# Two-layer network on one Trainium2 core: the experts' last layer as seven block products summed over the experts in PSUM

## The chip, the cores and the metric

The kernel runs on one core of one Trainium2 chip, in float32 throughout. The metric is the device time of one execution in microseconds (us), as the median of several runs; smaller is better. A profiled execution gives the times of single instructions on the five engines: PE (TensorE, matrix products; PEld is its weight load), DVE (VectorE), ACT (ScalarE), POOL (GpSimd) and SP (SyncE, which issues transfers). Matrix products land in PSUM, eight banks of 2 KB per partition; VectorE and ScalarE read them there, and everything else lies in SBUF.

## The reference

The input x is 32 x 128 tokens of 256 numbers (4096 tokens). Layer 0 adds a masked attention over all tokens with eight heads. Layer 1, where the change lies, is this:

```python
t = t + attention_in_a_window_of_24(layernorm(t), K)
t = t + experts(layernorm(t))

def experts(x):                                    # batch of one
    w = softmax(x @ Wr + br)                       # 8 shares per token
    h = relu(bn1(einsum('bfd,edh->bfeh', x, W1) + b1))
    h = relu(bn2(einsum('bfeh,ehk->bfek', h, W2) + b2))
    y = einsum('bfeh,ehd->bfed', h, Wo) + bo
    return einsum('bfed,fe->bfd', y, w)            # shares times outputs, summed
```

All eight experts see every token, so each of them is three products with a 256 x 256 matrix, and the last product is weighted by the token's share and summed over the experts.

## The kernel before

**Three stages.** Up to about 743 us runs layer 0's attention (scores L1257, exponentials L1269 and L1271, products L1301, sums L1291). From 743 to 790 us a front written out by hand (lines 2099 to 2203) brings the first block of 512 tokens through layer 1's attention: output projection of layer 0 in two halves (`first_halves`, `second`, `complete`), normalisation, turning, keys, window scores, exponentials, weights, `apply`/`attended`, the second normalisation (`expert_tokens`, L1768), its turning (`turn_tokens`), the first plain layer (`layer_halves`), the router (`route`, L1793). `batch_norms` (L1746) makes the scales and shifts for the experts there; its first step is a square root on ScalarE and a reciprocal (L908, L909). From 790 us on run the experts.

**The expert stage.** The work is 64 units, eight blocks of 512 tokens times eight experts, with the expert in the inner loop: `work = [(b, e) ...]`. A unit has three layers. `Layer(0, ...)` and `Layer(1, ...)` (L1887) hold channels on the partitions and tokens along the free axis. From unit PLAIN = 3 on each is done as a 2 x 2 block product with seven products instead of eight (Strassen's form with fifteen sums): `first()` issues four products of 128x128 by 128x256 into two PSUM banks, a and q (L1898), then a copy on ScalarE (u, L1924) and three additions on VectorE (L1925, L1926, L1927); `last()` adds three more products into the same banks, a relu from bank a on ScalarE (L1883), one addition on VectorE from bank q (L1940, 128x512), and two relus on ScalarE. The sums of weights come from GpSimd (`weight_sums`, L1540) during the first block, are stored to DRAM (`kept_sums`) and loaded again for later blocks (L1524). The sums of tokens for the second layer are three additions on VectorE (`token_sums`, L1873, L1877, L1878), called between the first layer's `last()` and the second layer's.

**The last layer.** `combine(ht, k, r2)` (L1947) is called twice a unit. It uses the second layer's output as weights, so that tokens land on the partitions: four products of 128x128 by 128x256 on TensorE into one bank psy (L1955), then two additions on VectorE that multiply a tile of 128 tokens by its share and add it to the token's residual in SBUF (`scalar_tensor_tensor`, L1963). The last expert's call sends the tile out.

**Order.** The main loop (L2359) writes, for unit k: the loads for unit k + 2 on SyncE's queue; first layer of unit k + 1, `first()`; half a combine; second layer of unit k, `first()`; `last()` of the first layer; half a combine; the token sums; `last()` of the second layer. After each piece `insert(passed)` (L2327) puts up to three jobs of later blocks: projections with a bias (`with_bias`, L904, on GpSimd), statistics, normalisation, turning, keys, scores, exponentials, routing, shares, biases. A job has a cost in TensorE time and due times spread over SPAN = E * 9.5 us a block; it comes LATER = 3.2 us of planned time after what it needs. Each engine runs its instructions in the order in which they were written.

**PSUM in this stage.** ps_h has four banks (two layers' a and q), ps_x four (jobs and combine):

```python
ps_h = ctx.enter_context(tc.tile_pool(name="ps_h", bufs=4, space=PSUM))
ps_x = ctx.enter_context(tc.tile_pool(name="ps_x", bufs=4, space=PSUM))
```

**Tokens.** Blocks 4 to 7 of the input are loaded early into tiles of their own (pool `res`) and held.

Of the kernel before, what the change touches and what calls it, by code (L numbers as in the profile page):

```python
# [823 lines left out]
def fast_kernel(ctx: ExitStack, tc: tile.TileContext, ins: dict, out: bass.AP, narrow):  # L824
# [92 lines left out]
    last_parts = []  # L917
    with ExitStack() as l0:
# [296 lines left out]
        with ExitStack() as at:  # L1215
# [4 lines left out]
            ps_a = scores_ps.enter_context(tc.tile_pool(name="ps_a", bufs=1, space=PSUM))  # L1220
            ps_b = scores_ps.enter_context(tc.tile_pool(name="ps_b", bufs=2, space=PSUM))
            ps_av = scores_ps.enter_context(tc.tile_pool(name="ps_av", bufs=1, space=PSUM))
# [160 lines left out]

            stat_at = {
# [17 lines left out]
            for n in range(len(steps) + LAG + 1 + 16):  # L1402
# [22 lines left out]
                if 0 <= n - LAG < len(steps):  # L1425
                    product(*steps[n - LAG])
                    bb, gg, jj = steps[n - LAG]
                    if jj == orders[bb][-1]:
                        ends = bb, gg
                        later.setdefault(n + 1, []).append((close_sums, ends))  # L1430
                        if ends != LASTU:
                            later.setdefault(n + 6, []).append((invert, ends))
                            later.setdefault(n + 12, []).append((scale, ends))
# [46 lines left out]
    res = ctx.enter_context(tc.tile_pool(name="res", bufs=1))  # L1480
# [7 lines left out]


    one_a = ps_a.tile([P, BLK], F32, tag="a", name="one_a")  # L1490
    one_b = ps_av.tile([P, BLK], F32, tag="av", name="one_b")
    three_a, three_b = (
        ps_b.tile([P, HG - 1, BLK], F32, tag="b", name=f"three{k}") for k in range(2)
    )
    ps_h = ps_x = None

    def open_banks():
        nonlocal ps_h, ps_x
        scores_ps.close()
        ps_h = ctx.enter_context(tc.tile_pool(name="ps_h", bufs=4, space=PSUM))  # L1500
        ps_x = ctx.enter_context(tc.tile_pool(name="ps_x", bufs=4, space=PSUM))
# [8 lines left out]
    w12, s12, wo, kept_sums = {}, {}, {}, {}  # L1510
# [15 lines left out]
    def load_last(k):  # L1526
        wo[k] = wf.tile([P, 2, D], F32, tag="wo", name=f"wo_{k}")
        expert_weights(wo[k], "Wo", work[k][1])

    def weight_sums(e):  # L1530

        t = s12[e] = wf.tile([P, 4, 2, P], F32, tag="s12", name=f"s12_{e}")
        a11, a21, a12, a22 = (
            w12[e][:, :, c, m * P : (m + 1) * P] for c in range(2) for m in range(2)
        )
        for k, (p, q, op) in enumerate((
            (a21, a22, ALU.add), (t[:, 0], a11, ALU.subtract),
            (a11, a21, ALU.subtract), (a12, t[:, 1], ALU.subtract),
        )):
            nc.gpsimd.tensor_tensor(t[:, k], p, q, op=op)  # L1540
        kept_sums[e] = wdr.tile([P, 4, 2, P], F32, name=f"kept{e}")
        nc.sync.dma_start(out=kept_sums[e], in_=t)

    Ksb = l1c.tile([P, 2, D], F32, name="Ksb")
    nc.sync.dma_start(out=Ksb, in_=ins["L1_attn_K"].rearrange("(c p) e -> p c e", p=P))
    load_tokens(4, res.tile([P, TPB, D], F32, name="tokens4"))
# [14 lines left out]
    def load_rest():  # L1561
        load_tokens(TPB + 1, res.tile([P, TPB, D], F32, name=f"tokens{TPB + 1}"))
        load_layers(1)
        for b in range(TPB + 2, NBLK):
            load_tokens(b, res.tile([P, TPB, D], F32, name=f"tokens{b}"))
# [7 lines left out]
    def deviations(ts, part):  # L1573
# [8 lines left out]
        nc.vector.reciprocal(rstd0[:, cols], rstd0[:, cols])  # L1582
        nc.vector.scalar_tensor_tensor(
# [10 lines left out]
    def project_half(n, c, ps, start):  # L1594
        nc.tensor.matmul(
            ps, lhsT=big_t[:, c, SIDE + n * P : SIDE + (n + 1) * P], rhs=woT[:, c, :],
            start=start, stop=(c == 1), skip_group_check=True,
        )

    def project(n):  # L1600
        ps = bank(f"pso{n}")[:, :D]
        for c in range(2):
            project_half(n, c, ps, not c)
        finish(n, ps)
        if n + TPB < NTILE:
            with_bias(n + TPB)
# [92 lines left out]
    def turn_weights(p, ps=None):  # L1699
# [11 lines left out]
        nc.vector.tensor_copy(pt[: 4 * SIDE, 2, :], ps[: 4 * SIDE, 2 * P : 3 * P])  # L1711
# [33 lines left out]

    def batch_norms():  # L1746
        def bnp(s):
            k = bn_names.index(s) * 2 * E
            return bnT[:, :, k : k + 2 * E]

        rstd_of(bscale, bnp("v"), 1e-3)
# [35 lines left out]
    def route(b):  # L1787

        xfT = blk[b]["xfT"]
        ps = bank(f"psr{b}")[:, :P]  # L1790
# [36 lines left out]
    def turn_shares(b):  # L1827
        ps = bank(f"pswt{b}")[:, :P]
        nc.tensor.transpose(ps, blk[b]["wide"].rearrange("p r e -> p (r e)"), ident)
        blk[b]["wT"] = fx.tile([P, P], F32, tag="wT", name=f"wT{b}", bufs=1)  # L1830
        nc.vector.tensor_copy(blk[b]["wT"], ps)
# [38 lines left out]
    def token_sums(x, tag, name):  # L1870

        t = fh.tile([P, 4, HB], F32, tag=tag, name=name)
        nc.vector.tensor_tensor(  # L1873
# [3 lines left out]
        nc.vector.tensor_tensor(t[:, 2], x[:, 1, HB:], t[:, 0], op=ALU.subtract)  # L1877
        nc.vector.tensor_tensor(t[:, 3], x[:, 1, :HB], t[:, 2], op=ALU.subtract)  # L1878
# [8 lines left out]
    class Layer:  # L1887
# [21 lines left out]
        def first(self):  # L1909
# [8 lines left out]
            self.product(a[:, 0], w[:, 0, :P], x[:, 0, :HB], True)  # L1918
            self.product(q[:, 0], s[:, 0], t[:, 0], True)
            self.product(a[:, 1], s[:, 1], t[:, 2], False)  # L1920
# [25 lines left out]

    def combine(ht, k, r2):  # L1947
        b, e = work[k]
        w = blk[b]["w"]
        dst = out[0].rearrange("n t d -> (n t) d")  # L1950
# [9 lines left out]
        for i in range(2):  # L1960
# [6 lines left out]
            if e == E - 1:  # L1967
                nc.sync.dma_start(out=dst[n * P : (n + 1) * P], in_=tokens(n))
# [11 lines left out]
    def bound_squares(name):  # L1980
        squares[name] = l1c.tile([P, 2, D], F32, tag="sq", name=f"sq_{name}", bufs=2)
        nc.gpsimd.tensor_tensor(squares[name], bound_of[name], bound_of[name], op=ALU.mult)
# [113 lines left out]
    def half(ps, k):  # L2096
        return ps[:, k * D : (k + 1) * D]

    def first_halves(n, ps, k):

        project_half(n, 0, half(ps, k), not k)


    places = [
        (one_a, 0), (one_a, 1), (one_b, 0), (one_b, 1),
        (three_a[:, 0], 0), (three_a[:, 0], 1), (three_a[:, 1], 0), (three_a[:, 1], 1),
    ]
    for n, (ps, k) in enumerate(places):
        first_halves(n, ps, k)

    def second(n):
        project_half(n, 1, half(*places[n]), False)

    def complete(n):
        finish(n, half(*places[n]))

    invert_last, scale_last = last_parts
    second(0)
# [9 lines left out]
    second(4)  # L2128
    complete(4)
# [10 lines left out]
    warm(one_b, 20)  # L2140
# [10 lines left out]
    complete(TPB + 1)  # L2151
    complete(TPB + 2)

    three_b = ps_b.tile([P, HG - 1, BLK], F32, tag="b", name="three_b")
    for n, (ps, k) in enumerate(((1, 0), (1, 1), (2, 0), (2, 1)), 2 * TPB):
        places.append((three_b[:, ps], k))

    def both(n):
        first_halves(n, *places[n])
# [3 lines left out]
    rows = [(one_a, 0), (one_a, 1), (three_b[:, 0], 0), (three_b[:, 0], 1)]  # L2163
    seen = [scores1(i, half(*rows[i])[:, :BW]) for i in range(TPB)]
    for n in range(2 * TPB + 1, 3 * TPB):
        both(n)
    for i in range(TPB):
        seen[i]()
        exponentials(i)
        if i == 1:  # L2170
            turn_weights(0, one_b)
    complete(2 * TPB - 1)
    attended = apply(0, [one_a[:, :D], one_b[:, :D]])
    turn_weights(1, three_a[:, 0])
    batch_norms()
    attended(0)
    attended(1)
    deviations(range(0, 2), 0)
    attended = apply(1, [one_a[:, :D], one_b[:, :D]])
    deviations(range(0, 2), 1)  # L2180
    expert_tokens(0, 0)
    turn_tokens(0, 0, three_a[:, 1])
    attended(0)
    attended(1)
    deviations(range(2, TPB), 0)
    a = layer_halves(blk[0]["xfT"], [one_b, three_a[:, 0]])
    next(a)
    deviations(range(2, TPB), 1)
    expert_tokens(0, 1)
    turn_tokens(0, 1, one_a)  # L2190
# [3 lines left out]
    a = next(a)  # L2194
    open_banks()
    deviations(groups[1], 1)
    route(0)
    first_free = 3 * TPB
    for n in range(first_free, first_free + TPB):
        with_bias(n)  # L2200
# [11 lines left out]
    for n in groups[0]:  # L2212
        done_at["normalise", n] = done_at["turn", n] = -9
    for g in (0, 1):
# [9 lines left out]
    for b in range(1, NBLK):  # L2224
        ts = groups[b]
        for n in ts:
            job(("project", n), 0.86, lambda n=n: project(n))
# [29 lines left out]
        job(("devt", b), 0, lambda b=b: deviations(tiles(b), 1), ("devt0", b))  # L2257
# [16 lines left out]
        if b == 2:  # L2274
            two_ahead = {"wV": "wc", "K": "wK"}
            for name in bound_of:
                job(
                    ("square", name), 0, lambda name=name: bound_squares(name),
                    *((("columns", two_ahead[name]),) if name in two_ahead else ()),
                )  # L2280
# [21 lines left out]
    SPAN = E * 9.5  # L2302
# [4 lines left out]
    for name, cost, f, needs in jobs:  # L2307
        own = isinstance(name, tuple) and isinstance(name[1], int)
        b = name[1] if own else 2
        if own and name[0] in ("project", "normalise", "turn"):  # L2310
# [16 lines left out]
    def insert(passed):  # L2327

        nonlocal now, spent
        now += passed  # L2330
# [16 lines left out]
    known = set(done_at) | {j[0] for j in jobs}  # L2347
# [3 lines left out]
    h1, h2 = {0: (a, None)}, {}  # L2351
    halves = [(k, r2) for k in range(len(work)) for r2 in range(2)]
    sums_of = {0: (0, 1), 1: (2, 3)}

    def combine_half():
        k, r2 = halves.pop(0)
        combine(h2[k], k, r2)

    for k in range(len(work)):  # L2359
        if k + 2 < len(work):  # L2360
            load_layers(k + 2)
        load_last(k)
        if k + 2 < E:
            for e in sums_of.get(k, (k + 2,)):
                weight_sums(e)
        one = None
        if k + 1 < len(work):
# [5 lines left out]
            insert(1.73)  # L2373
        if k >= 2:
            combine_half()
            insert(1.73)
        two = Layer(1, k, *h1.pop(k))
        two.first()
        insert(1.73)
        if one:  # L2380
            one.last()
# [59 lines left out]
```

## Time and profile before

| what | value |
|---|---|
| median of 3 runs | 1539.02 us (1538.96 to 1543.28) |
| profiled execution, time | 1543.32 us |
| profiled execution, span on the core | 1541.5 us |
| granted TensorE clock, mean | 0.991 |
| TensorE busy | 1484.6 us, 8877 instructions |
| bytes moved | 110.16 MB, mean 71 GB/s |

The span is the profiled execution's own; 1.8 us lie around it. Busy times of engines overlap. A product of 128x128 by 128x256 in float32 shows as two instructions of 0.38 us that overlap, so its slot is read from the distance of starts, not from the mean duration. A row of the timeline names the start, the time until the last of its instructions ended, the engine, the line, the operation, output and inputs, and, in brackets, for how long the engine had been idle and which instruction ended that. Line numbers are those of the kernel before.

### The profile page before, as it was taken

How to read it: one execution, taken by the hardware profiler on the slowest of the kernel's cores; microseconds unless marked ns; L12 is line 12 of the kernel's file. 1: busy time of each engine (PE TensorE's matmuls, PEld its weight loads, DVE VectorE, ACT ScalarE, POOL GpSimd, SP SyncE). 2: the span in 40 equal slices, each digit the busy share in tenths (PEclk: the TensorE clock that was granted, in tenths of full speed). 3: DMA queues.
4: the chain of work that ended last, by engine and by line, in shares of the span. 5: the costliest groups of instructions: out<-in, count | busy, mean ns of one | idle time of the engine just before them, and what ended most of it. 6: DMA issues, size and time to landing. Idle time of an engine off the chain costs nothing.

```text
span 1541.5 us, 23828 instructions
## 1 busy us (share of the span) xinstructions
PE 1484.6 (96%) x8877; PEld 840.7 (55%) x8877; DVE 1204.5 (78%) x2203; ACT 937.4 (61%) x1393; POOL 162.0 (11%) x380
## 2 busy tenths in 40 slices
PE   8899899999999999999889999999999999999998
PEld 5333232222222222222547878887877888888887
DVE  3677888989999898999647778677777777777775
ACT  3676687878888888988444445545454444544443
POOL 1111003000000000031053002001010010000000
PEclk8999999999999999999989999999999999999999
DMA  4211101010000010000322333343333433343441
GB/s 117 56 31 27 39 8 31 8 29 9 1 15 8 1 49 15 8 9 1 115 79 93 116 117 106 115 139 107 116 107 112 141 107 117 106 141 111 137 151 64
DMA packets 95976, 110.16 MB, mean 71 GB/s; under 512 B 17527, under 2 KB 84846, under 8 KB 95854
## 3 DMA queue, kind: packets, MB, share of 16 engines
q1 hardware_dynamic: 93008, 106.61, 22.4%
q8 instruction: 72, 1.18, 0.3%
q10 hardware_dynamic: 1150, 1.09, 0.3%
q0 software_dynamic: 1696, 0.87, 0.2%
q14 instruction: 50, 0.41, 0.1%
HBM read 98.87 MB, written 8.53 MB: 70 GB/s over the span
## 4 chain that ended last, share of the span: by engine, by line
PE 72%; DVE 15%; ACT 8%; issue 4%; DMA 0%; POOL 0%; DVEq 0%; ACTq 0%; SPq 0%; POOLq 0%
PE psh L1898 17%; PE sa L1257 14%; PE av L1301 13%; PE psy L1955 10%; DVE acc L1291 3%; ACT h L1883 3%; ACT pt L1271 2%; PE psq L995 2%; PE psv L1010 2%; PE psk L982 2%; PE psk L1654 2%; DVE h L1940 1%; PE sb L1257 1%; DVE tokens L1963 1%; PE psh L1903 1%
## 5 line engine op out<-in xcount | busy, mean ns | idle before, releaser
L1291 DVE TENSOR_TENSOR acc<-acc,pt 128x1024 f32<-128x1024 f32 (+3 forms) x500 | 529.4, 1126 | 40.0 <-ACT pt L1271 28.7
L1271 ACT ACTIVATE pt<-sb 128x1536 f32<-128x1536 f32 (+3 forms) x288 | 387.3, 1345 | 3.3 <-PE sb L1257 3.2
L1257 PE MATMUL sa<-q,kT 32*128 32x512 f32 (+3 forms) x576 | 302.2, 604 | 9.4 <-ACT pt L1269 7.1
L1257 PE MATMUL sb<-q,kT 32*128 32x512 f32 (+3 forms) x1728 | 306.1, 604 | 2.2 <-ACT pt L1271 1.1
L1883 ACT ACTIVATE h<-h,bshift,bscale 128x256 f32<-128x256 f32 x244 | 159.2, 699 | 231.6 <-DVE h L1940 231.6
L1301 PE MATMUL av<-pt,v 128*32 128x512 f32 (+3 forms) x2304 | 286.2, 569 | 3.1 <-POOL pt L1275 1.6
L1955 PE MATMUL psy<-wo,h 128*128 128x256 f32 x1024 | 242.9, 380 | 0.0
L1269 ACT ACTIVATE pt<-sa 128x512 f32<-128x512 f32 (+3 forms) x288 | 162.5, 564 | 92.7 <-PE sb L1257 63.1
L1955 PEld LDWEIGHTS psy<-wo,h 128*128 128x128 f32 x1024 | 191.9, 190 | 30.7 <-issue 5.8
L1257 PEld LDWEIGHTS sa<-q,kT 32*128 32x128 f32 x576 | 84.2, 182 | 220.1 <-ACT pt L1269 180.0
L1301 PEld LDWEIGHTS av<-pt,v 128*32 128x32 f32 x2304 | 45.4, 108 | 202.2 <-issue 182.8
L1963 DVE SCALAR_TENSOR_TENSOR tokens<-psy,w,tokens 128x256 f32<-128x256 f32 x256 | 111.1, 475 | 34.2 <-PE psy L1955 33.7
L1925 DVE TENSOR_TENSOR u<-psh,u 128x256 f32<-128x256 f32 x122 | 51.1, 419 | 101.3 <-ACT u L1924 101.2
L1275 POOL MEMSET pt<- 32x128 f32 (+2 forms) x192 | 58.6, 305 | 635.2 <-ACT pt L1271 541.2
L1883 ACT ACTIVATE h<-psh,bshift,bscale 128x256 f32<-128x256 f32 (+1 forms) x132 | 75.9, 575 | 55.5 <-PE psh L1898 41.3
L1257 PEld LDWEIGHTS sb<-q,kT 32*128 32x128 f32 x1728 | 88.0, 182 | 10.2 <-ACT pt L1271 6.8
L1924 ACT COPY u<-psh 128x256 f32<-128x256 f32 x122 | 44.1, 362 | 78.6 <-PE psh L1898 78.5
L1898 PE MATMUL psh<-tx,s 128*128 128x256 f32 x366 | 89.3, 380 | 0.0
L1898 PE MATMUL psh<-th,s 128*128 128x256 f32 x366 | 89.0, 379 | 0.0
L1940 DVE TENSOR_TENSOR h<-psh,u 128x512 f32<-128x512 f32 x122 | 83.1, 681 | 1.5 <-PE psh L1898 1.4
L1898 PEld LDWEIGHTS psh<-tx,s 128*128 128x128 f32 x366 | 69.2, 190 | 10.4 <-DVE h L1940 0.8
L1898 PEld LDWEIGHTS psh<-th,s 128*128 128x128 f32 x366 | 69.5, 190 | 9.5
(316 smaller groups left out, 1785.6 us busy)
## 6 DMA issues: line engine op xcount, KB each, us to landing
w<-in_L_ffn_W_dram SPq DMA_DIRECT2D x128, 256.0 KB
s<-kept SPq DMA_DIRECT2D x56, 512.0 KB
wo<-in_L_ffn_Wo_dram SPq DMA_DIRECT2D x64, 256.0 KB
xg<-in_x_dram SPq DMA_DIRECT2D x32, 128.0 KB
tokens<-in_x_dram SPq DMA_DIRECT2D x8, 512.0 KB
kept<-s SPq DMA_DIRECT2D x8, 512.0 KB
out_dram<-tokens SPq DMA_DIRECT2D x32, 128.0 KB
rec<-flat SPq DMA_DIRECT2D x60, 64.0 KB
```

Of the source, the lines that this page charges most:

```text
L1257: nc.tensor.matmul((sb[:, h - 1, :] if h else sa)[:, lo:], lhsT=kT[rows, g, j * P : (j + 1) * P], rhs=q[rows, g, lo:], start=True, stop=True,)
L1269: nc.scalar.activation(pt[:, 0, lo:], sa[:, lo:], AF.Exp, scale=SCALE)
L1271: nc.scalar.activation(pt[:, 1:, lo:], sb[:, :, lo:], AF.Exp, scale=SCALE)
L1275: nc.gpsimd.memset(pt[k * N : (k + 1) * N, :, lo : lo + k * N], 0.0)
L1291: nc.vector.tensor_tensor(live[b, g][:, hs, lo:], old[:, hs, lo:], pt[:, hs, lo:], op=ALU.add)
L1301: nc.tensor.matmul(av[h * HD : (h + 1) * HD, lo:], lhsT=v[:, j, (g * HG + h) * HD : (g * HG + h + 1) * HD], rhs=pt[:, h, lo:], start=(j == ...
L1883: nc.scalar.activation(dst, src, AF.Relu, bias=bshift[:, m, k : k + 1], scale=bscale[:, m, k : k + 1])
L1898: nc.tensor.matmul(ps, lhsT=w, rhs=x, start=start, stop=True, skip_group_check=True)
L1925: nc.vector.tensor_tensor(u, a[:, 1], u, op=ALU.add)
L1940: nc.vector.tensor_tensor(flat.rearrange("p (k c) -> p k c", k=2), self.q, self.u.unsqueeze(1).to_broadcast([P, 2, HB]), op=ALU.add,)
L1955: nc.tensor.matmul(ps[:, i, :], lhsT=ht[:, c, r * P : (r + 1) * P], rhs=wo[k][:, c, :], start=(c == 0), stop=(c == 1),)
L1963: nc.vector.scalar_tensor_tensor(out=tokens(n), in0=ps[:, i, :], scalar=w[:, r, e : e + 1], in1=tokens(n), op0=ALU.mult, op1=ALU.add,)
```

## The change

For units 0 to 61 (SUMMED = 62) the last layer becomes a 2 x 2 block product of seven products too, and its eight experts are summed in PSUM:

- **Shares first.** The shares are written to DRAM per block, and for every unit one row is broadcast to all partitions (`load_shares`, SyncE). GpSimd multiplies the second layer's output by it (`shared`: two products of 128x512) and makes the three token sums.
- **Seven products a unit**, issued one at a time by `product()`, up to four between the four pieces of a unit's order (`between`), into four banks that stay for a whole block (`ps_y`). The sums of Wo's blocks are made once by VectorE (`last_sums`) and reloaded later.
- **Once per block** `close_block` forms the four quarters from the seven sums (one ScalarE copy, six VectorE additions), and `turn_out` turns the result back to tokens on the partitions (eight transposes), adds the residual and sends it out. Units 62 and 63 keep `combine`.
- **PSUM:** ps_h goes from 4 banks to 2, ps_x from 4 to 2, ps_y gets 4. In `first()` the second product of bank a now comes before the first of bank q.
- **Order:** `one.first, between, one.last, between, two.first, between, two.last, between`; SPAN = E * 9.05; `with_bias` becomes a job; blocks 4 to 7 of the input are loaded again when a block's output is out (`load_again`), in place of `res`.
- **Front:** first halves of the projections are issued ahead of the last product of layer 0; table loads are called up by a one-element activation (`ready`); `batch_norms` is split and later; routing and the first layer come before the completions of tiles 8 to 11; 16 warming transposes in place of 20; only one `with_bias` ahead of the stage.

```diff
+        ps_h = ctx.enter_context(tc.tile_pool(name="ps_h", bufs=2, space=PSUM))
+        ps_x = ctx.enter_context(tc.tile_pool(name="ps_x", bufs=2, space=PSUM))
+        ps_y = ctx.enter_context(tc.tile_pool(name="ps_y", bufs=1, space=PSUM))
...
             self.product(a[:, 0], w[:, 0, :P], x[:, 0, :HB], True)
+            self.product(a[:, 1], s[:, 1], t[:, 2], False)
             self.product(q[:, 0], s[:, 0], t[:, 0], True)
-            self.product(a[:, 1], s[:, 1], t[:, 2], False)
             self.product(q[:, 1], s[:, 2], t[:, 1], False)
...
+    def shared(k):
+        b, e = work[k]
+        wb = blk[b].pop(("wb", e))
+        for c in range(2):
+            nc.gpsimd.tensor_tensor(h2[k][:, c, :], h2[k][:, c, :], wb, op=ALU.mult)
+        return h2[k], token_sums(h2[k], "ty", f"ty{k}", nc.gpsimd)
+    def last_products(k):
...
+        for i, j, lhs, rhs in (
+            (0, 0, w[:, 0, :P], x[:, 0, :HB]), (0, 1, w[:, 1, :P], x[:, 1, :HB]),
+            (1, 0, s[:, 3], x[:, 1, HB:]), (1, 1, s[:, 0], t[:, 0]),
+            (2, 1, s[:, 2], t[:, 1]), (2, 0, s[:, 1], t[:, 2]),
+            (3, 0, w[:, 1, P:], t[:, 3]),
+        ):
+            first = not e and (i, j) in ((0, 0), (1, 0), (2, 1), (3, 0))
+            nc.tensor.matmul(
+                y[i][:, j], lhsT=lhs, rhs=rhs, start=first, stop=True, skip_group_check=True
+            )
+            yield
+    def turn_out(b, r2):
+        ps = bank(f"psc{b}_{r2}")
...
+        nc.vector.tensor_tensor(t, ps.rearrange("p (k d) -> p k d", d=D), t, op=ALU.add)
...
+    SHARED, SUMS = 5.0, 7.5
+    def product(forced=False):
...
+        if not forced and now < second_done[k] + (SHARED if i < 3 else SUMS):
+            return False
...
+    def between():
+        product()
+        insert()
+        begin_shared()
+        product()
...
             one.first()
-            insert(1.73)
-        if k >= 2:
-            combine_half()
-            insert(1.73)
+            passed(1.73)
+            if k:
+                between()
+            one.last()
+            passed(1.3)
+            between()
         two = Layer(1, k, *h1.pop(k))
         two.first()
-        insert(1.73)
-        if one:
-            one.last()
-            insert(1.3)
-        if k >= 1:
-            combine_half()
-            insert(1.73)
...
+        between()
         two.last()
...
+        second_done[k] = now
+        between()
```

## The prediction

> **What bounds the kernel now.** I first read the busy shares, then the windows by stage, then the groups of instructions, and last the rows of the expert stage one by one. The first view says which engine is nearest to full:
>
> ```profile
> PE 1484.6 (96%) x8877; PEld 840.7 (55%) x8877; DVE 1204.5 (78%) x2203; ACT 937.4 (61%) x1393; POOL 162.0 (11%) x380
> ```
>
> An average over stages does not price an edit to one stage, so I cut the span where the work changes. The columns are stretch, length, PE, PEld, DVE, ACT, POOL (busy us), granted clock, DMA share, GB/s.
>
> ```profile
> 743.00:790.00 47.00, 36.34 (x177) 25.83 (x176) 31.08 (x98) 14.81 (x32) 9.48 (x17) 0.89 0.31 102
> ...
> 828.50:1425.80 597.30, 589.49 (x2874) 487.13 (x2874) 450.92 (x1191) 278.09 (x561) 45.74 (x102) 1.00 0.36 117
> 1425.80:1514.00 88.20, 87.58 (x407) 75.66 (x406) 64.06 (x148) 40.78 (x76) 0.00 (x0) 1.00 0.44 144
> ```
>
> The first stretch is the hand-written front; the second holds 50 expert units with the next blocks' jobs between them (597.3 / 50 = 11.95 us each); the third has almost no jobs. In both expert stretches PE idles about 1%: TensorE bounds them. A unit without jobs is 22 passes: in the trace a unit's first product starts at 1504.06 and the next unit's at 1513.56, so 9.50 / 22 = 0.432 us a pass. The groups that the change touches:
>
> ```profile
> L1955 PE MATMUL psy<-wo,h 128*128 128x256 f32 x1024 | 242.9, 380 | 0.0
> L1963 DVE SCALAR_TENSOR_TENSOR tokens<-psy,w,tokens 128x256 f32<-128x256 f32 x256 | 111.1, 475 | 34.2 <-PE psy L1955 33.7
> ```
>
> **What TensorE alone would gain.** Units 0 to 61 need seven passes in place of eight: 62 x 0.432 = -26.8 us. Turning eight blocks back adds 64 transposes; four such transposes take 0.43 us in the same stage of this trace, so 64 x 0.109 = +7.0. Net -19.8 us, if TensorE stays the bound.
>
> **What the change takes for it.** The four running sums of a block need four PSUM banks for eight units. So Layer's pool ps_h falls from four banks to two, and one layer needs both. In the changed issue order the next layer's third product (bank q) waits for the sum L1940 of the layer before, and ScalarE's copy L1924 of the next layer stands behind the two relus that wait for that same sum. With four banks two layers are in flight; with two, each layer follows the one before through a closed loop TensorE, VectorE, ScalarE, VectorE. Its links can all be timed in the trace of before, in the tail where nothing else is queued (start, length, engine, operation, idle time before it and what ended it):
>
> ```profile
> 1495.78 0.69 DVE L1940 TENSOR_TENSOR h<-psh,u 128x512 f32<-128x512 f32 x1
> ...
> 1496.50 1.30 ACT L1883 ACTIVATE h<-h,bshift,bscale 128x256 f32<-128x256 f32 x2 [2.00 <-DVE h L1940]
> 1497.71 0.35 ACT L1924 COPY u<-psh 128x256 f32<-128x256 f32 x1
> ...
> 1498.09 0.42 DVE L1925 TENSOR_TENSOR u<-psh,u 128x256 f32<-128x256 f32 x1 [1.63 <-ACT u L1924]
> ...
> 1498.62 0.42 DVE L1926 TENSOR_TENSOR h<-psh,u 128x256 f32<-128x256 f32 x1
> 1499.08 0.42 DVE L1927 TENSOR_TENSOR h<-psh,h 128x256 f32<-128x256 f32 x1
> ```
>
> From the start of L1940 to the end of L1927 are 1499.50 - 1495.78 = 3.72 us. TensorE follows VectorE within about 0.05 us, where it does wait:
>
> ```profile
> 1124.54 0.42 DVE L1927 TENSOR_TENSOR h<-psh,h 128x256 f32<-128x256 f32 x1
> ...
> 1125.02 0.70 PE L1898 MATMUL psh<-xfT,s 128*128 128x256 f32 x2 [0.29 <-DVE h L1927]
> ```
>
> Then come the layer's last two products and the handover to L1940: 0.43 + 0.59 + 0.04 = 1.06 us. The loop is 3.72 + 0.05 + 1.06 = 4.83 us a layer, two layers a unit: 9.66. In every second layer VectorE has the three sums of L1873, L1877 and L1878 between L1927 and L1940; they take 1.52 us (1503.76 to 1505.28) in a gap of 1.11, so +0.41. **A unit without jobs becomes 10.07 us**, against 9.50 before and 21 x 0.432 = 9.07 by TensorE alone.
>
> The Trainium skill ("Perfetto Trace Analysis", section "Matmuls") says independent matmul groups should rotate through PSUM banks so that evacuation of one overlaps the next group's matmuls. The rule speaks against this change, with two groups' banks cut to one's; it gives no price, and no run here yet shows it.
>
> **With jobs between.** TensorE's own need is 11.95 - 0.43 + 0.11 (turning back) = 11.63 us a unit. The loop lengthens by every job operation that stands on ScalarE between relus and copy, or on VectorE between L1927 and L1940. Counted in the issue order of the changed kernel, over 103 layers of units 4 to 55 and by durations of before's rows: 30 us of ScalarE operations (a 128x256 normalise 0.55, exponentials, copies) with some 8 us of table loads (1.28 each); on VectorE 89 us beyond the gaps, of which 21 are the 0.41 above. So 9.66 + (30 + 8 + 89) / 51.5 = 12.1 us. That is a mean; a layer takes the longer of loop and TensorE's passes, which are unevenly spread (4.3 to 6.5 us a layer). Taking the longer one layer by layer, with the same durations, gives 644 / 51.5 = 12.5. Ends: 11.6 (all of it beside other work, TensorE the bound) and 12.7 (every such operation also delays its neighbour). I take **12.35**: 50 x (12.35 - 11.95) = **+20 us**. Nine units without jobs: 9 x 0.57 = **+5**.
>
> **VectorE and GpSimd.** VectorE loses 248 of the L1963 (0.435 each in pairs, 108 us) and gains a block's closing (six operations, some 2.8 us) and eight sums of the last weights. The 108 us were idle cover, not the bound; this gain counts at nothing but for the loop, where it is already left out. GpSimd gets two products of 128x512 and three sums per unit. From its rows (queried by line):
>
> ```profile
> L1982 POOL TENSOR_TENSOR sq_wV<-wVT 128x512 f32<-128x512 f32 x1 | 1.1, 1053 | 0.0
> L1540 POOL TENSOR_TENSOR s<-w,s 128x256 f32<-128x256 f32 x6 | 4.4, 730 | 0.0
> ```
>
> 3 x 1.05 + 2 x 0.73 = 4.6 us of a unit's 10 to 12, where it now does next to nothing: it fits, and the last layer's products are ordered at least 5 us (7.5 for the sums) behind. But one pair of rows shows VectorE losing beside it, an operation of one element per partition at 1.04 us, and 0.16 alone (814.85):
>
> ```profile
> 818.99 1.05 POOL L1982 TENSOR_TENSOR sq_wV<-wVT 128x512 f32<-128x512 f32 x1
> 819.70 1.04 DVE L1690 TENSOR_TENSOR nm<-nm,negt 128x1 f32<-128x1 f32 x1
> ```
>
> VectorE's loop operations read PSUM, and L1963 kept its 0.47 beside the same GpSimd row (820.66). The three sums read SBUF alone, but GpSimd works from 2 to 6.6 us after the second layer's L1940 and the sums stand 8 to 10 us after it. Cost taken: 0; ends 0 and 0.88 x 62 = +55.
>
> The Trainium skill ("SBUF — State Buffer", section "Who interferes with whom") says a VectorE operation with two SBUF inputs and a GpSimd operation that reads SBUF exclude each other for the whole instruction. By it, the sums meeting a GpSimd operation of 1.05 in each of 62 units would make up to +65; the 1.04 us row agrees with the rule.
>
> **DMA.** 62 broadcasts of shares (256 KB) and some 54 reloads of kept sums (256 KB) add 30 MB to 750 us, 40 GB/s to today's 117 at a share of 0.36: near 0.5, no bound. SyncE's queue takes two more issues of 0.4 to 0.9 us a unit. Tokens of blocks 4 to 7 come again only after a block's output has left; with_bias may wait for them on GpSimd with the xh transfers and the share products behind it. Taken 0; ends 0 and 4 x 5 = +20.
>
> **Front.** TensorE idles 10.4 us between 743 and 790, in nine gaps. The largest, 2.79 (until 773.59, behind batch_norms and its table load) and 2.71 (until 789.09, routing behind four completions), are what the reorder removes; two pairs of L1768 took 1.61 and 1.77 beside GpSimd instead of 0.8, about 1.8 more; an earlier table load 0.9. Sum 8.2: **-8**, ends 0 and -12. **End:** the turning back of block 7 and its VectorE closing stand before the last outputs: 0.9 + 2.1 = **+3**, ends 0 and 5. Units 0 to 3 I take at 0, ends -3 and +3.
>
> **Sum.** +20 + 5 - 8 + 3 = +20 on the profiled execution's 1543.3 (span 1541.5 and 1.8 around it), so 1563. That execution was the slowest of its kind, 4.3 above the median 1539.0; on the median's scale the forecast is **1559**.
>
> **Rivals.**
> - *TensorE stays the bound* (faster): where a unit's jobs add under 11.63 - 10.07 = 1.56 us to the loop, the passes hide it. For it: jobs are many, and TensorE needs 11.63 itself. Against: counted, they add 2.1. Then 50 x -0.32 = -16, +5, -8, +3: 1523; if the bare loop also hides, -20 - 8 + 1: 1512.
> - *GpSimd becomes the wait* (slower still): collisions at half the upper price, +28, or products waiting for shares: 1580 to 1600. Against: 4.6 us of 10 and the distance kept.
> - *Nothing to measure*: the loop costs 12.0 us a unit and the front pays for it: 1535 to 1543.
>
> **How the numbers follow.** Forecast (loop-bound; 1544 to 1578 with 12.1 to 12.6 a unit and a front of 0 to -12) 0.56; GpSimd 0.11; no change 0.07; TensorE-bound 0.26. About 0.3% is what a measurement can tell from no change. Faster 0.26, same 0.07, slower 0.67. The range for 8 in 10 reaches 1516 to 1590.
>
> **What would show it.** In the tail without jobs: units of 10.1 us, TensorE waiting for L1927's and L1940's successors twice a unit, copies right behind relus, PE near 90%. If units are 9.1 there, the loop is wrong. With jobs: units over 12 us, PE near 94%. GpSimd's rival shows as products waiting on POOL, or sums over 1 us. The front is right if the first layer product comes 8 us earlier than 789.67 less what stage one moved.

## The result and the profile after

The changed kernel takes 1624.32 us in the median of four runs (1620.61 to 1627.78), the kernel before 1539.45 beside it: 1.0541 times as long, with a 95% interval of 1.0522 to 1.056. The forecast was 1559, the range 1516 to 1590: the side was right, the size too small by 65 us, and the time lies outside the range. The profiled execution took 1620.6 us, its span is 1618.8, so 77.3 more than before's span.

The busy shares of the kernel after:

```profile
PE 1511.1 (93%) x8813; PEld 824.5 (51%) x8813; DVE 1175.5 (73%) x2041; ACT 943.2 (58%) x1404; POOL 487.7 (30%) x691
```

TensorE has 64 instructions fewer and is busy 26.5 us longer. That is the first thing to see here: its work takes more time per instruction. To find where, I cut both traces at four marks that both have: the first layer product of the stage, and the last addition (L1940 before, L1978 after) of the second layer of units 10, 54 and 62. The windows of after, then of before (stretch, length, then PE, PEld, DVE, ACT and POOL busy, granted clock, DMA share, GB/s):

```profile
780.32:961.20 180.88, 152.20 (x632) 107.95 (x633) 109.17 (x280) 67.80 (x133) 90.61 (x107) 0.91 0.37 121
961.20:1515.20 554.00, 519.88 (x2427) 407.74 (x2426) 359.55 (x884) 248.35 (x497) 264.95 (x306) 0.99 0.48 155
1515.20:1599.60 84.40, 79.95 (x341) 62.82 (x340) 46.10 (x97) 35.00 (x66) 41.77 (x40) 0.98 0.51 166
```

```profile
789.67:931.10 141.43, 138.82 (x641) 104.89 (x638) 94.89 (x264) 65.92 (x132) 34.08 (x66) 0.99 0.32 105
931.10:1447.80 516.70, 510.30 (x2483) 422.92 (x2482) 390.59 (x1026) 245.71 (x491) 31.80 (x68) 1.00 0.37 118
1447.80:1524.30 76.50, 76.50 (x356) 67.36 (x355) 54.18 (x122) 34.16 (x64) 0.00 (x0) 1.00 0.41 135
```

The account: the stage starts 9.4 us earlier (780.32 for 789.67); up to unit 10 it then loses 180.9 - 141.4 = 39.5; the next 44 units lose 554.0 - 516.7 = 37.3, the last eight 7.9; the end 2.0. Sum -9.4 + 39.5 + 37.3 + 7.9 + 2.0 = 77.3. In the first stretch the 39.5 are 26.1 us more of idle TensorE (28.7 for 2.6) and 13.4 more of busy TensorE (152.2 for 138.8), at a granted clock of 0.91 for 0.99. In the second stretch it is idle 34.1 us (before 6.4).

More than half of the first loss is there by the second layer of unit 3. Its last addition, before and after:

```profile
842.57 0.68 DVE L1940 TENSOR_TENSOR h<-psh,u 128x512 f32<-128x512 f32 x1
```

```profile
855.61 0.69 DVE L1978 TENSOR_TENSOR h<-psh,u 128x512 f32<-128x512 f32 x1 [2.55 <-PE psh L1936]
```

From the first layer product these are 52.9 us before and 75.3 after: 22.4 us of the 39.5. Units 4 to 10 lose the other 17.1.

The steady loop is the one the prediction timed. Rows of after, job-free, from one last addition to the next (start, length, engine, operation; in brackets the idle time before and what ended it):

```profile
1579.33 0.68 DVE L1978 TENSOR_TENSOR h<-psh,u 128x512 f32<-128x512 f32 x1
...
1580.05 1.30 ACT L1921 ACTIVATE h<-h,bshift,bscale 128x256 f32<-128x256 f32 x2 [1.75 <-DVE h L1978]
...
1581.27 0.35 ACT L1962 COPY u<-psh 128x256 f32<-128x256 f32 x1
...
1581.64 0.42 DVE L1963 TENSOR_TENSOR u<-psh,u 128x256 f32<-128x256 f32 x1 [1.63 <-ACT u L1962]
...
1583.11 0.70 PE L1936 MATMUL psh<-xfT,s 128*128 128x256 f32 x2
...
1584.28 0.69 DVE L1978 TENSOR_TENSOR h<-psh,u 128x512 f32<-128x512 f32 x1 [1.22 <-PE psh L1936]
...
1589.47 0.68 DVE L1978 TENSOR_TENSOR h<-psh,u 128x512 f32<-128x512 f32 x1
```

4.95 us for this layer, 5.19 for the next with its token sums: 10.14 a unit where 10.07 was worked out. The copy starts as the relus end (1581.27, and 1580.05 + 1.30 = 1581.35). Eight such units would be 81.1; the last stretch is 84.4, since block 6 is closed in two of its units (12.19 and 11.37 us). The first block is another matter:

```profile
804.40 2.48 POOL L2001 TENSOR_TENSOR h<-h,wb 128x512 f32<-128x512 f32 x2 [5.42 <-DMA wb<-sh]
...
805.72 1.22 PE L2020 MATMUL y<-h,wo 128*128 128x256 f32 x2 [5.35 <-POOL h L2001]
...
817.12 2.57 POOL L2001 TENSOR_TENSOR h<-h,wb 128x512 f32<-128x512 f32 x2
817.23 1.35 DVE L1564 TENSOR_TENSOR so<-wo,so 128x128 f32<-128x128 f32 x1
818.49 1.75 DVE L1911 TENSOR_TENSOR tx<-xfT 128x512 f32<-128x512 f32 x1
...
820.27 1.37 DVE L1915 TENSOR_TENSOR tx<-xfT,tx 128x256 f32<-128x256 f32 x1
...
821.70 2.93 PE L1936 MATMUL psh<-tx,s 128*128 128x256 f32 x6 [5.87 <-DVE tx L1915]
```

The same two token sums before:

```profile
814.93 0.68 DVE L1873 TENSOR_TENSOR tx<-xfT 128x512 f32<-128x512 f32 x1
...
815.65 0.42 DVE L1877 TENSOR_TENSOR tx<-xfT,tx 128x256 f32<-128x256 f32 x1
```

GpSimd waits for the broadcast shares, TensorE for GpSimd; then VectorE's sums, 0.28 (the sum of weights, as at 815.56), 0.68 and 0.42 us elsewhere, take 1.35, 1.75 and 1.37 beside GpSimd, and TensorE waits 5.87 us for them. In the window around these rows the granted clock is 0.62:

```profile
803.00:830.00 27.00, 17.72 (x53) 12.30 (x54) 13.72 (x30) 1.71 (x3) 13.88 (x14) 0.62 0.26 82
```

### The profile page after: what moved, and what is told of

The parts are those of the page before. It is cut to its first block, busy times and chain, and to the rows that moved or that the text cites. A ratio compares the mean times of both kernels' runs of the same rounds, so it can differ in the third digit from the quotient of the medians.

```text
span 1618.8 us, 24127 instructions
## 1 busy us (share of the span) xinstructions
PE 1511.1 (93%) x8813; PEld 824.5 (51%) x8813; DVE 1175.5 (73%) x2041; ACT 943.2 (58%) x1404; POOL 487.7 (30%) x691
## 4 chain that ended last, share of the span: by engine, by line
PE 58%; DVE 22%; ACT 12%; issue 5%; POOL 2%; DMA 1%; DVEq 0%; SPq 0%; ACTq 0%; POOLq 0%
PE sa L1258 14%; PE av L1302 13%; PE psh L1936 11%; PE y L2020 5%; ACT h L1921 5%; DVE h L1978 3%; DVE acc L1292 2%; DVE h L1964 2%; DVE h L1965 2%; DVE u L1963 2%; PE psq L996 2%; ACT pt L1272 2%; PE psv L1011 2%; PE psk L983 2%; PE sb L1258 1%
## 5 line engine op out<-in xcount | busy, mean ns | idle before, releaser
L2001 POOL TENSOR_TENSOR h<-h,wb 128x512 f32<-128x512 f32 x124 | 155.6, 1276 | 327.1 <-ACT h L1921 314.1
L1963 DVE TENSOR_TENSOR u<-psh,u 128x256 f32<-128x256 f32 x122 | 51.6, 423 | 161.5 <-ACT u L1962 161.0
L1978 DVE TENSOR_TENSOR h<-psh,u 128x512 f32<-128x512 f32 x122 | 83.2, 682 | 47.8 <-PE psh L1936 47.6
L2020 PE MATMUL y<-ty,so 128*128 128x256 f32 x372 | 108.4, 386 | 0.0
L1936 PE MATMUL psh<-tx,s 128*128 128x256 f32 x366 | 93.0, 387 | 8.9 <-DVE tx L1915 5.9
L1936 PE MATMUL psh<-th,s 128*128 128x256 f32 x366 | 92.5, 383 | 8.5 <-DVE h L1978 8.4
L1936 PE MATMUL psh<-xfT,w 128*128 128x256 f32 x244 | 75.6, 391 | 11.3 <-DVE u L1963 11.0
L1936 PE MATMUL psh<-h,w 128*128 128x256 f32 x244 | 76.2, 394 | 7.6 <-DVE u L1963 5.6
L1911 POOL TENSOR_TENSOR ty<-h 128x512 f32<-128x512 f32 x62 | 79.5, 1283 | 4.9
```

Source lines behind the costliest of these rows:

```text
L1911: eng.tensor_tensor(t[:, 0:2], x[:, :, HB:], x[:, 0, :].rearrange("p (k c) -> p k c", k=2), op=ALU.subtract,)
L1936: nc.tensor.matmul(ps, lhsT=w, rhs=x, start=start, stop=True, skip_group_check=True)
L1963: nc.vector.tensor_tensor(u, a[:, 1], u, op=ALU.add)
L1978: nc.vector.tensor_tensor(flat.rearrange("p (k c) -> p k c", k=2), self.q, self.u.unsqueeze(1).to_broadcast([P, 2, HB]), op=ALU.add,)
L2001: nc.gpsimd.tensor_tensor(h2[k][:, c, :], h2[k][:, c, :], wb, op=ALU.mult)
L2020: nc.tensor.matmul(y[i][:, j], lhsT=lhs, rhs=rhs, start=first, stop=True, skip_group_check=True)
```

## The experiments

The kernel before was measured again beside each group of runs; its median lay between 1539.8 and 1542.7. Times below are medians, ratios to the kernel before with their 95% intervals. Where a time at a mark is compared between traces, it is counted from the stage's first layer product, since that product comes between 776.7 and 781.6 us in the versions with the changed kernel's front.

**1 and 2. Order or banks?** The prediction blamed two banks. Both kernels are the kernel before in the changed order of layers; the second has two banks for the layers.

```diff
             one.first()
             insert(1.73)
+            one.last()
+            insert(1.3)
         if k >= 2:
             combine_half()
...                                  # one.last() and the second half of combine leave this place
         two.last()
...
+        if k >= 1:
+            combine_half()
-        ps_h = ... bufs=4            # second kernel only
+        ps_h = ... bufs=2
```

> The kernel before with the changed order of layers (first() and last() of a layer follow each other, one layer in flight) and everything else as before: four banks, combine, its shares on VectorE. If the order makes the loop (theory A: ScalarE's copy of the next layer stands behind the relus of this one, whatever the banks), a unit without jobs takes 10.0 to 10.2 us instead of 9.50 and the whole 1560 to 1600. If the banks make it (theory B: with four banks TensorE runs ahead), the unit stays at 9.5 to 9.6 and the whole within 8 us of 1539.

> The same with two banks for the layers in place of four. Theory A: within 6 us of the run with four banks, unit without jobs again 10.0 to 10.2. Theory B: 1560 to 1600, and 20 us or more above the run with four banks.

Measured: 1669.6 us (1.0841, 1.0822 to 1.0859) with four banks, 1669.1 (1.0833, 1.0815 to 1.0851) with two. In this serial order the two banks cost nothing: theory B falls. The size was missed in both: 130 us in place of 20 to 60, and 12.1 us a job-free unit. The rows of the run with four banks show why:

```profile
1601.19 1.89 PE L1955 MATMUL psy<-wo,h 128*128 128x256 f32 x8
1601.40 0.69 DVE L1940 TENSOR_TENSOR h<-psh,u 128x512 f32<-128x512 f32 x1 [1.22 <-PE psh L1898]
1602.12 1.30 ACT L1883 ACTIVATE h<-h,bshift,bscale 128x256 f32<-128x256 f32 x2 [1.58 <-DVE h L1940]
...
1602.92 0.59 PE L1898 MATMUL psh<-h,w 128*128 128x256 f32 x2
...
1604.42 0.37 ACT L1924 COPY u<-psh 128x256 f32<-128x256 f32 x1 [0.99 <-PE psh L1898]
```

Here the copy does not stand behind the relus, it waits for TensorE: half a combine (1.73 us) stands between one layer's last product and the next layer's first, and the relus are over before the copy's input is there. So this loop is not the changed kernel's, where the copy waits for the relus: the two runs show that a serial order is dear and that four banks do not mend it, and not yet which link closes the loop of the changed kernel. Run 3 shows that.

In the first block the order has a price without any of the new work: up to unit 10 run 1 takes 152.4 us and run 2 154.4 where before takes 141.4, all of it lost in units 4 to 10 (up to unit 3 both take 52.7, before 52.9).

**3. The loop opened.** The two relus of a layer are issued behind the next layer's copy (and one of the places where share products may be issued is dropped).

```diff
             nc.scalar.copy(u, a[:, 0])
+            finish_held()          # the two relus of the layer before
...
-            relu(out[:, 0, HB:], out[:, 0, HB:], self.l, e, 0)
-            relu(out[:, 1, :], out[:, 1, :], self.l, e, 1)
+            held.append((out, self.l, e))
```

> The changed kernel, with the two last relus of a layer issued on ScalarE behind the copy of the next layer (and the share products' first chance to be issued moved behind it). The loop then runs from the sum over the third and fourth product to the last addition, about 0.72 + 0.05 + 1.06 + 0.42 + 0.05 + 1.06 = 3.4 us a layer, under TensorE's 4.53. Theory A and B alike: units without jobs 9.1 to 9.5 us instead of 10.1, the whole 1570 to 1600 instead of 1624. If the loop is not what holds the steady part back (rival: waits for shares and for reloaded tokens do), less than 10 us are won.

Measured: 1577.32 us (1.0242, 1.0225 to 1.0259), 47 less than the changed kernel, from little more than the order of two instructions on ScalarE. Job-free:

```profile
1535.48 0.68 DVE L1988 TENSOR_TENSOR h<-psh,u 128x512 f32<-128x512 f32 x1
...
1536.53 0.37 ACT L1971 COPY u<-psh 128x256 f32<-128x256 f32 x1 [1.97 <-PE psh L1944]
1536.80 1.30 ACT L1921 ACTIVATE h<-h,bshift,bscale 128x256 f32<-128x256 f32 x2
...
1544.58 0.68 DVE L1988 TENSOR_TENSOR h<-psh,u 128x512 f32<-128x512 f32 x1
```

The copy now comes first. From 1535.48 to 1544.58 are 9.1 us a unit, and in the window of four such units TensorE is busy all the time:

```profile
1516.60:1553.90 37.30, 37.30 (x172) 31.26 (x172) 22.10 (x45) 17.47 (x33) 20.93 (x20) 1.00 0.52 165
```

So two banks are enough for a unit without jobs. From unit 10 to unit 62 the time falls from 638.4 to 601.0; up to unit 10 from 180.8 to 173.2. With jobs the two banks do show: half of TensorE's idle time between these marks (20.2 us in this run) stands before a product that waits for the addition of the layer before to empty bank q. The wait in this run, then in the changed kernel, where 1.3 us of it stand before other products (us in total, times, longest):

```profile
PE psh L1944 <- DVE h L1988: 10.1, 10, 1.5
```

```profile
PE psh L1936 <- DVE h L1978: 11.3, 14, 3.0
```

Run 1, with four banks, has no such wait. What four banks would give the changed kernel was not measured; with ps_y's four there is no room for them.

**4. Waits for reloaded tokens.** GpSimd waited four times, 17.1 us in all, for tokens loaded again.

```diff
-                    ends.append((("load", b + TPB), 0, lambda: load_again(b + TPB), outs))
+                    ends.append((("again", c), 0, lambda: load_again(c), outs))
+                    for name, after in ("l1", "again"), ("l2", "l1"), ("load", "l2"):
+                        ends.append(((name, c), 0, lambda: None, ((after, c),)))
```

> The changed kernel, with the bias additions of blocks 4 to 7 planned 6.4 us later behind the reload of their tokens, so that GpSimd does not stand waiting for the transfer (four waits of up to 5.0 us, 17 in all, with the share products behind them). If these waits make the steps of 9, 4, 7 and 5 us seen at four places of the trace, the whole falls by 15 to 25 us to 1600 to 1609; if something else does, it stays within 5 us of 1624.

Measured: 1629.63 us (1.0579, 1.0555 to 1.0604), no gain. The four waits are gone from GpSimd's list, the time is not. The edit also moves jobs: units 11 to 20 took 11.7 us longer, which could hide what the first two waits cost. From unit 21 to 62, where the other two had held GpSimd for 9.7 us, it gained 1.0.

**5. The first block without shares.** Combine for units 0 to 7, the seven products from unit 8 on.

```diff
+    START = E
-        if k < SUMMED:
+        if START <= k < SUMMED:
             to_load.append(k)
...
+            if 0 < k <= START:
+                combine(h2[k - 1], k - 1, 0)
```

> The changed kernel, with the old combine for units 0 to 7 (the whole first block), the seven products from unit 8 on. Theory: the first block loses some 39 us (first layer product 9.4 us earlier than before, the layers of unit 12 then 30 us later) to the trip of the shares through DRAM, to GpSimd's share products that stand between the weight sums there, to VectorE's sums beside them (0.42 us sums at 0.8 to 1.7), and to the half clock after each stall. Without shares in that block 20 to 30 us come back: 1594 to 1604. Rival: the serial order and the jobs make it, then less than 8 us come back.

Measured: 1624.05 us (1.0536, 1.0513 to 1.0559): nothing came back, and the expected 20 to 30 were wrong: it is the rival's case that came. Up to the second layer of unit 3 it takes 71.3 us in place of 75.3, up to unit 10 179.3 in place of 180.8, and later nothing is left. TensorE is idle as long as with the shares (28.0 us). So the trip of the shares alone does not make the slow first block. Combine has a price of its own here, a pass more per unit (8 x 0.432 = 3.5 us) and waits of TensorE for its additions in the two banks that the jobs use; how far that hides a gain was not separated.

**6. The clearing of the routing tile.** In the trace after, VectorE waits at three of the seven routings from 790 us on for one instruction of 0.2 us, 11.7 us in all. The longest of the three:

```profile
1309.64 0.20 POOL L1841 MEMSET w<- 128x128 f32 x1
...
1309.88 0.19 DVE L1844 TENSOR_TENSOR w<-psrt,br 128x32 f32<-128x32 f32 x1 [5.87 <-POOL w L1841]
...
1311.17 1.13 PE L1936 MATMUL psh<-th,s 128*128 128x256 f32 x4 [2.96 <-DVE h L1978]
```

It stands behind a unit's share work on GpSimd (5.2 us), VectorE's job waits for it, the layer's addition stands behind that job, and TensorE waits for the addition. The window just after shows half clock:

```profile
1313.00:1316.00 3.00, 3.00 (x5) 1.04 (x4) 2.56 (x6) 1.71 (x3) 0.00 (x0) 0.50 0.03 5
```

```diff
-        nc.gpsimd.memset(wide, 0.0)
+        nc.vector.memset(wide, 0.0)
```

> The changed kernel, with the clearing of the routing tile (one 0.2 us instruction a block) on VectorE instead of GpSimd, where it stands behind the share products of a unit. Theory: VectorE's waits for it (11.7 us in all, the longest 5.9, each held the layer's last addition up and is followed by half clock) go, and 8 to 20 us with them: 1604 to 1616. Rival: the next wait takes over, under 4 us.

Measured: 1615.57 us (1.0473, 1.0455 to 1.049), 8.8 less: the cause is there, at the low end. In the traces the changed kernel loses 4.9 us against this run between units 36 and 38, where the row above stands.

**7. The front alone**, on the kernel before (the diff is that of the change's front, its expert stage left as it was).

> The kernel before with the changed front alone (projections begun earlier, table loads called up, batch_norms split, routing and first layer ahead of the completions, 16 warming transposes); the expert stage is that of before. The prediction's front term was -8, the trace after shows the first layer product 9.4 us earlier. If the gain lasts to the end: 1529 to 1533. If the jobs and GpSimd's order at the start of the stage give it back: 1536 to 1540.

Measured: 1538.77 us beside 1542.7, ratio 0.9973 (0.9963 to 0.9983): 4 us faster, less than the 8 forecast. The figure lies in the second expected range, but not for its reason: the stage gives nothing back. The trace has the first layer product at 783.40 (6.3 earlier, not 9.4: it waits 3.97 us for the additions that empty the front's banks) and every mark from unit 3 on some 5.5 to 6.1 us earlier. This is the only version that beats both kernels.

**8 to 11. Repairs together.** The eighth kernel joins the edits of 3, 5 and 6; the ninth gives its first block's combine the four idle banks of ps_y; the tenth moves the sums of the last weights to GpSimd; the eleventh has the edits of 3 and 6 alone.

```diff
+        if k < START:                                    # ninth and tenth
+            ps = ps_y.tile([P, 2, D], F32, tag=f"y{(2 * k + r2) % 4}", ...)
-        block_sums(nc.vector, t, ...)                    # tenth
+        block_sums(nc.gpsimd, t, ...)
```

> The changed kernel with three repairs: relus behind the next copy, combine in the first block, the clearing on VectorE. If the three causes are apart, the gains add: 1577 - 25 - 12 = 1540, 1530 to 1552. If they overlap, 1555 to 1570.

> The kernel with three repairs, with the combine of the first block in the four banks that the running sums do not need yet, so that ps_x's two banks serve jobs alone there. In the run with three repairs TensorE waited in the first 170 us of the stage some 9 us for additions that empty ps_x (combine's and apply's). Theory C (two job banks are a cause of the slow first block): 1562 to 1570 after 1577. Rival (serial order and VectorE's queue make it): 1574 to 1580.

> The run before this one, with the sums of the last layer's weights on GpSimd instead of VectorE, so that VectorE's queue in the first block is that of the kernel before. Theory D (these sums, at 0.28 to 1.35 us each beside GpSimd, stand in the layers' loop): 5 to 12 us less than the run before this one. Rival: GpSimd's own weight sums become late instead, no gain within 3 us.

> The changed kernel with two repairs only: relus behind the next copy, and the clearing on VectorE. If the two causes add: 1577 - 9 = 1565 to 1571. If the shorter loop already covers the wait for the clearing: 1574 to 1579.

Measured: 1576.7 us (1.0231, 1.0208 to 1.0253), 1574.6 (1.0208, 1.0163 to 1.0252), 1567.95 (1.0176, 1.0144 to 1.0208) and 1580.2 (1.0241, 1.0224 to 1.0258). The gains do not add. Clearing on VectorE is worth 8.8 us with the closed loop and nothing with the open one: in the trace of run 3 VectorE no longer waits for the clearing at all. The banks for jobs are not shown to matter in the time (2 us within a wide interval; up to unit 10 the ninth takes 167.3 us, the eighth 173.2). For the sums of the last weights the medians fall by 6.7 us, but the two intervals overlap. The traces point the same way: 167.3 to 160.6 up to unit 10, with TensorE's one long wait for VectorE's sums down from 5.1 to 2.7 us and the clock up from 0.96 to 0.99. So theory D is likely, with its size open: runs 3 and 11, which differ only in where the clearing is done, lie 4.0 us apart at the same mark (173.2 and 177.2). The first stretch of the tenth kernel:

```profile
780.00:940.90 160.90, 143.08 (x645) 103.32 (x643) 103.24 (x275) 67.96 (x136) 66.68 (x118) 0.99 0.37 123
```

The clock is 0.99 again; 17.8 us of TensorE's idle time are left, mostly short waits for VectorE.

**12. GpSimd's share.** Shares multiplied into one column only; the rest of the output goes without them.

```diff
-        for c in range(2):
-            nc.gpsimd.tensor_tensor(h2[k][:, c, :], h2[k][:, c, :], wb, op=ALU.mult)
+        nc.gpsimd.tensor_tensor(h2[k][:, 0, :1], h2[k][:, 0, :1], wb[:, :1], op=ALU.mult)
```

> The changed kernel, with the shares multiplied into one column of the second layer's output only (left out: the shares of the other columns, so the output is not the experts' weighted sum); transfers, sums, order and banks are as in the changed kernel. It takes 2.5 us a unit (155 in all) off GpSimd. Theory A (the order of layers, and VectorE's and ScalarE's queues in it): 5 to 15 us less, 1609 to 1619, as the clearing and the first block's weight sums stand less long behind GpSimd. Rival (GpSimd is the wait of the steady part): over 30 us less, under 1594.

Measured: 1602.9 us (1.0415, 1.0392 to 1.0437), 21 less: between the two expectations. In the traces, 9.2 us of it come up to unit 10 (180.8 to 171.6), another 9.7 by unit 38 (VectorE's waits for the clearing fall from 11.7 us to 6.0), and none after; the rest is an earlier start of the stage (3.6). Job-free units stay at 10.14. The token sums of the first layers, once a block and slowed to 0.90 us for their first in the changed kernel, are back at 0.68 here. GpSimd is no wait of the job-free loop; it is one of the first block and of what stands behind it.

## Why the prediction was wrong, point by point

- *TensorE alone gains 19.8.* Seven products and 64 transposes came as counted, but the gain was paid back in waits and clock: even with the loop open (run 3), the time from unit 10 to unit 62 is 601.0 us where before takes 593.2, with TensorE idle for 20.2 us in place of 6.4.
- *The loop, 10.07 us without jobs.* Right: 10.14, and its links were right, as run 3 shows by cutting one of them. Its wording blames too much on the banks: runs 1 and 2 agree within 1 us, and run 3 fills TensorE with two banks. What closes the loop is the order, with first and last of a layer side by side and the relus ahead of the copy; the banks are a reason for that order, and by themselves show only with jobs (the 10 us under run 3).
- *With jobs, 12.35 a unit; +20 and +5.* Mis-sized: 44 units lost 37.3 us where 44 x 0.40 = 17.6 were forecast, and the last eight 7.9 for 8 x 0.57 = 4.6 (3.3 us of them for closing block 6). It left out that a job which waits holds the loop (the clearing, 8.8 us) and that a long stall is followed by a lower clock. It also took VectorE's jobs at before's durations, and beside the busier GpSimd some grew: the normalisation of the experts' tokens (L1768, now L1803) from 0.41 to 0.61 us on the mean, a sum of one element per partition behind the scores (L1690, now L1720) from 0.23 to 0.42. In run 12 they are 0.48 and 0.19. How much of the loss comes from this was not separated.
- *Front -8:* -9.4 in its place; made alone, 6.3 in the trace and 4 in the medians. *End +3:* +2.0. *DMA 0 and reloads 0:* no gain from taking the waits away.
- *Units 0 to 3 at 0, ends -3 and +3, and GpSimd at 0.* **This is the step that failed**: up to unit 10 the loss is 39.5 us, 22.4 of them up to unit 3, where 0 was put, and 17.1 in units 4 to 10, which the sum had at 0.40 each. I read GpSimd's fit from its idle share in the steady part and its order from the steady distances; in the first block it still makes weight sums, the shares come through DRAM just in time, and VectorE makes the last weights' sums beside it. Its work was mis-sized too: 4.6 us a unit forecast, 5.2 measured, as a product of two different tensors took 1.28 us where the row of a square had 1.05. Differences up to unit 10, on different kernels: relus 7.6, GpSimd's share products 9.2, the last weights' sums 6.8, and the clock, 0.91 for 0.99. They overlap, and leaving the shares out of the block altogether (run 5) gave 1.5: the tenth kernel still takes 160.6 us there against 141.4. The 19.1 that remain go with TensorE's waits, mostly for VectorE. The serial order alone costs 11.0 in run 1, in a longer loop than here; what part it, the job banks or the earlier due times have in the 19.1 stays open.
- *A misread row.* That L1963 kept its length beside the GpSimd product does not follow from the row at 820.66: that product (818.99, 1.05 us) had ended at 820.04.
- *Rivals.* That GpSimd would be the wait had 0.11 with 1580 to 1600; it was part of the truth: taking half of its new work away (run 12) gave 21 of 85 us back, 9.2 of them in the first block. None of the cases reached 1624, because each added one mechanism to the same steady unit; here several added up.

The rule cited from the Trainium skill ("SBUF — State Buffer", section "Who interferes with whom") was weighed for the wrong place: the 61 token sums of the second layers stayed near their old length (0.70, 0.43 and 0.43 us on the mean, 0.68 and 0.43 before), while those of the first layers, once a block, grew (0.90, 0.59 and 0.65 on the mean, 0.68 and 0.42 before), and run 12 has the first of them at 0.68 again. The rows of the first block (0.42 us at 1.37 beside GpSimd) agree with the rule.

## What to carry to other kernels

When a change takes buffers away, write down the order that the remaining ones force, and time the loop of one item around all engines; then look for the link that is only an order on one engine, since swapping two instructions there can be worth more than the products saved. When an idle engine gets work, list what else is queued on it, in the first block too, and who waits for the smallest of these instructions. Price a stall of TensorE of some 3 us with the half clock that followed it here.

## What the runs showed of the hardware

An idle stretch of 2.96 us on TensorE (until 1311.17) was followed by a granted clock of 0.50 in the window from 1313 to 1316. GpSimd's product of two different 128x512 tensors took 1.28 us on the mean, where squaring one took 1.05. Beside it VectorE's sum of two such tensors in SBUF took up to 1.75 us, 0.68 without.
